# A graph network kernel's prologue: weight loads behind adj and x, layernorm of batch 1 ahead of the branch, VectorE's work dealt anew

## The chip, the cores and the metric

The kernel runs on one core of a Trainium2 chip. The metric is the device time of one execution in microseconds (us). Before the change it was 1216.17 us, the median of three runs (1215.86 to 1218.9). All runs below are in the fast state. A ratio is the mean time of one kernel's fast runs divided by that of the other's fast runs of the same rounds on the same chip, with a 95% interval; it is therefore not quite the ratio of the medians quoted beside it.

Engines in the profile: PE is TensorE, PEld its weight loads, DVE VectorE, ACT ScalarE, POOL GpSimd, SP SyncE. "L442" is a line of that kernel's own source, so the same statement has another number in each kernel.

## The reference

There are 32 batches of x, each 512 rows by 512 features, and one 512x512 matrix adj, all fp32.

```python
# layer 0
h = jnp.maximum(_layernorm(x), 0.0)
x = x + (einsum('nm,bmd->bnd', adj, h) @ weight + bias)
# layer 1: attention, masked by (1 - adj) * -1e9, 8 heads
h = jnp.maximum(_layernorm(x), 0.0)
x = x + (softmax(scores + mask) @ v) @ Wo + bo
```

adj is sparse with values up to 1, so the mask is close to one-hot per row. The kernel finds the largest entry of each row of adj, checks with bounds from the weights that the softmax picks just that row, and then replaces attention by a gather of rows (the "single path"); otherwise it branches to a general path. The inputs here take the single path.

## The kernel before

The prologue runs before the branch. adj goes out in four chunks on SyncE's queue, batch 0 of x on ScalarE's, the weights right behind them on the same two queues, and three bias vectors on GpSimd's queue:

```python
for c in range(C):
    nc.sync.dma_start(mask[:, c, :], adj[c * P:(c + 1) * P, :])
    nc.scalar.dma_start(xs[0][:, c, :], x[0, c * P:(c + 1) * P, :])
# ... constants ...
for t, v in zip(bt, (bq, bk)):
    nc.gpsimd.dma_start(t, v.rearrange("(c p) -> p c", p=P))
nc.gpsimd.dma_start(b0_r, ...)          # bias, one row copied to 128 partitions
load_w(nc.scalar, wt[0], wq)
load_w(nc.sync, wt[1], wk)
load_w(nc.scalar, w0_s, w0)
load_w(nc.sync, xs[1], x[1])
load_w(nc.scalar, wv_s, wv)
load_w(nc.sync, wo_s, wo)
```

TensorE transposes the chunks of adj as they land, ScalarE and VectorE copy the transposes from PSUM, and then TensorE aggregates batch 0 over features (24 passes, two more products, the row counts). A check value decides the branch.

After the branch every 512x512x512 product is done as seven half-size pieces (Strassen's way), whose operand sums VectorE makes: h0s for the aggregation, yTs for layer 0. While TensorE works on one piece, a list of steps says what the other engines do. Batch 0's part of that list:

```python
for c in range(C):
    put(0, c, add_b0, c)
for step, i in ((0, 0), (0, 1), (0, 2), (1, 3)):
    put(0, step, lambda b, i: sum_b(adjT_s, adjT, i), i)
for step, c in ((1, 0), (1, 1), (2, 2), (2, 3)):
    put(1, step, lambda b, c: first[0].stats(c), c)      # layernorm of batch 1
put(1, 2, lambda b: first[0].power())
put(1, 3, lambda b: first[0].offset())
for c in range(C):
    put(1, 3, lambda b, c: first[0].relu(c), c)
for step, i in ((3, 0), (7, 1), (8, 2), (9, 3)):
    put(1, step, h0_sum, i)
# ... number_rows at 9, list_rows at 10 to 13, w0_t sums at 15 to 17 ...
run(layer0_rows(0), todo[0:4])            # batch 0, layer 0
run(aggregate(b + 1), todo[7:14])         # batch 1, aggregation in seven pieces
run(fold_weights(), todo[14:21])          # Wv x Wo
```

So the aggregation of batch 1 needs a layernorm, a ReLU and the sums h0s that VectorE makes only after the branch.

## Time and profile before

| | before |
|---|---|
| time, first three runs | 1216.17 us median |
| profiled span | 1217.6 us |
| TensorE busy | 1164.6 us, 96% of the span |
| aggregation of batch 0 starts | 12.71 us |
| first product after the branch (layer 0 of batch 0) | 31.71 us |
| layer 0 of batch 1 starts | 81.81 us |
| mean granted clock of TensorE | 0.988 |

TensorE is the bound, so only the time in which it waits, or in which it runs at half clock, can be won. The start of layer 0 of batch 1 is a good milestone: from there both kernels issue the same instructions in the same order, and a lead there should reach the end. The page's groups show the largest single wait of the one kind that the change attacks (columns: busy us, mean ns, idle before and its releaser):

```profile
L271 PE MATMUL mm<-adjT_s,h0s 128*128 128x256 f32 x744 | 171.0, 379 | 3.8 <-DVE h0s L248 3.2
```

Of 744 passes in 31 batches, one waits 3.2 us for h0s: only batch 1's.

### The profile page before, as it was taken

The numbers are of one execution on the slowest core, as the hardware profiler recorded it, in microseconds if no ns is written. First come the engines' busy times: TensorE is split into PE (matmuls) and PEld (weight loads), VectorE is DVE, ScalarE is ACT, GpSimd is POOL, SyncE is SP. The second block draws the span as 40 slices with busy tenths as digits, with TensorE's granted clock in tenths as the row PEclk, the third lists the DMA queues.
The fourth block names the chain that finished last, engine by engine and source line by source line (L and its number), as shares of the span: only waits on it lengthen the run. The fifth ranks groups of instructions, "written<-read, shape, count | busy, mean of one in ns | idle before, by whom it ended". The sixth has DMA issues, their size and how long they took to land.

```text
span 1217.6 us, 14536 instructions
## 1 busy us (share of the span) xinstructions
PE 1164.6 (96%) x5164; PEld 938.2 (77%) x5164; DVE 849.0 (70%) x1854; ACT 327.3 (27%) x499; POOL 401.9 (33%) x340
## 2 busy tenths in 40 slices
PE   7899999999999999999999999999999999999971
PEld 3458888888888888888888888888888888888841
DVE  4877776777777677777767777777777777777541
ACT  3223223222322322232232223223222322322110
POOL 1132432433233343324324332433433243343332
PEclk9999999999999999999999999999999999999986
DMA  8222665565566556556655655665565566555466
GB/s 284 78 61 91 169 169 147 152 188 167 152 169 167 149 152 186 169 152 167 167 149 152 185 170 152 168 168 148 152 186 170 153 166 171 144 152 153 135 162 149
DMA packets 97874, 192.43 MB, mean 158 GB/s; under 512 B 10624, under 2 KB 10624, under 8 KB 97792
## 3 DMA queue, kind: packets, MB, share of 16 engines
q1 hardware_dynamic: 69104, 127.95, 28.7%
q0 software_dynamic: 26528, 59.27, 26.6%
q10 hardware_dynamic: 2160, 4.19, 0.9%
q8 instruction: 42, 0.69, 0.2%
q14 instruction: 40, 0.33, 0.1%
HBM read 99.10 MB, written 92.28 MB: 157 GB/s over the span
## 4 chain that ended last, share of the span: by engine, by line
PE 86%; DVE 7%; DMA 1%; issue 1%; POOL 1%; ACT 0%; SPq 0%; POOLq 0%; DVEq 0%; ACTq 0%
PE mm L271 72%; PE mm L478 9%; PE pt L464 3%; DVE st L185 2%; DVE zs L482 2%; PE mm L352 1%; DVE zs L318 1%; DVE mv L186 1%; DMA hc<-hs,listed 1%; POOL x L488 0%; DMA z<-zs 0%; DVE x L422 0%; ACT h L199 0%; DVE x L445 0%; DVE yT L308 0%
## 5 line engine op out<-in xcount | busy, mean ns | idle before, releaser
L488 POOL DMA_INDIRECT x<-z,place x128 | 201.5, 1574 | 252.0 <-DMA z<-zs 209.6
L199 ACT ACTIVATE h<-x,off,rstd 128x512 f32<-128x512 f32 x256 | 194.7, 807 | 201.9 <-DVE off L195 201.9
L326 DVE TENSOR_TENSOR x<-mm,x 128x512 f32<-128x512 f32 x217 | 149.8, 690 | 119.1 <-PE mm L271 119.1
L192 POOL TENSOR_TENSOR rstd<-ve,mhalf 128x2 f32<-128x2 f32 (+1 forms) x97 | 88.2, 909 | 288.4 <-DVE ve L191 287.0
L185 DVE BATCH_NORM_STATS2 st<-x 128x6 f32<-128x512 f32 x256 | 175.3, 685 | 10.9 <-DMA x<-in_x_dram 8.7
L455 POOL DMA_INDIRECT hc<-hs,listed x96 | 102.8, 1071 | 235.3 <-PE mm L271 177.5
L271 PE MATMUL mm<-adjT_s,h0s 128*128 128x256 f32 x744 | 171.0, 379 | 3.8 <-DVE h0s L248 3.2
L271 PE MATMUL mm<-w_t,sel 128*128 128x256 f32 x744 | 171.0, 379 | 1.2 <-DVE x L326 1.2
L271 PEld LDWEIGHTS mm<-adjT_s,h0s 128*128 128x128 f32 x744 | 141.2, 190 | 23.6 <-issue 4.5
L271 PEld LDWEIGHTS mm<-w_t,sel 128*128 128x128 f32 x744 | 138.9, 190 | 19.1 <-DVE x L326 1.6
L465 ACT COPY hT<-pt 128x512 f32<-128x512 f32 x96 | 56.5, 588 | 356.3 <-PE pt L464 356.3
L310 ACT COPY yT<-mm 128x512 f32<-128x512 f32 x124 | 72.7, 586 | 266.2 <-PE mm L271 222.1
L478 PE MATMUL mm<-wvo,hT 128*128 128x512 f32 x256 | 116.8, 599 | 0.7 <-ACT hT L465 0.7
L271 PE MATMUL mm<-adjT,h 128*128 128x256 f32 x496 | 117.3, 379 | 0.0
L271 PE MATMUL mm<-w_s,yT 128*128 128x256 f32 x496 | 117.2, 379 | 0.0
L308 DVE TENSOR_TENSOR yT<-mm,yT 128x512 f32<-128x512 f32 x93 | 64.3, 692 | 75.2 <-PE mm L271 72.9
L271 PE MATMUL mm<-wvo_t,hTs 128*128 128x256 f32 x384 | 104.2, 395 | 6.5 <-DVE zs L318 6.2
L271 PEld LDWEIGHTS mm<-w_s,yT 128*128 128x128 f32 x496 | 94.2, 190 | 13.2 <-issue 0.5
L271 PEld LDWEIGHTS mm<-adjT,h 128*128 128x128 f32 x496 | 94.1, 190 | 13.3 <-ACT h L199 0.6
L271 PEld LDWEIGHTS mm<-wvo_t,hTs 128*128 128x128 f32 x384 | 67.9, 189 | 32.5 <-DVE zs L318 24.9
L478 PEld LDWEIGHTS mm<-wvo,hT 128*128 128x128 f32 x256 | 49.2, 193 | 49.5 <-issue 46.9
L422 DVE TENSOR_TENSOR x<-x,b_r 128x512 f32<-128x512 f32 x128 | 87.3, 683 | 0.0
(131 smaller groups left out, 1309.1 us busy)
## 6 DMA issues: line engine op xcount, KB each, us to landing
hs<-h SPq DMA_DIRECT2D x64, 512.0 KB
out_dram<-x SPq DMA_DIRECT2D x128, 256.0 KB
x<-in_x_dram SPq DMA_DIRECT2D x120, 256.0 KB
z<-zs SPq DMA_DIRECT2D x96, 256.0 KB
x<-z,place POOLq DMA_INDIRECT x128
hc<-hs,listed POOLq DMA_INDIRECT x96
x<-in_x_dram ACTq DMA_DIRECT2D x4, 256.0 KB
mask<-in_adj_dram SPq DMA_DIRECT2D x4, 256.0 KB
```

Of the source, the lines that this page charges most:

```text
L185: self.nc.vector.bn_stats(st, self.src[:, self.chunks[i], :])
L192: self.nc.gpsimd.tensor_tensor(self.rstd, ve, self.mhalf[:, 0:n], ALU.pow)
L199: self.nc.scalar.activation(self.dst[:, c, :], self.src[:, c, :], AF.Relu, bias=self.off[:, i:i + 1], scale=self.rstd[:, i:i + 1])
L271: nc.tensor.matmul(bank[:, m, :], lhs[:, k, m * P:(m + 1) * P], rhs[:, k, :], start=(first and m == 0 and k == 0), stop=(k == 1), skip_gro ...
L308: nc.vector.tensor_add(dst, bank, dst)
L310: nc.scalar.copy(dst, bank)
L326: nc.vector.tensor_add(dst, bank, dst)
L422: nc.vector.tensor_add(X[b][:, c, :], X[b][:, c, :], b0_r)
L455: nc.gpsimd.indirect_dma_start(out=HC[b][:, r, :], out_offset=None, in_=HS[b], in_offset=bass.IndirectOffsetOnAxis(ap=listed[:, r:r + 1], ...
L465: nc.scalar.copy(HT[b][:, :, r * P:(r + 1) * P], pt)
L478: nc.tensor.matmul(flat, HT[b][:, d, 2 * P:3 * P], wvo[:, d, :], start=(d == 0), stop=(d == DC - 1))
L488: nc.gpsimd.indirect_dma_start(out=X[b][:, c, :], out_offset=None, in_=Z[b], in_offset=bass.IndirectOffsetOnAxis(ap=place[:, c:c + 1], axi ...
```

## The change

Its intent has three parts. Part 1 holds the weight loads back behind adj and x and puts them all on ScalarE's queue. Part 2 does batch 1's layernorm ahead of the branch, where VectorE is idle. Part 3 deals VectorE's work after the branch anew.

```diff
-        load_w(nc.scalar, wt[0], wq)
-        load_w(nc.sync, wt[1], wk)
-        load_w(nc.scalar, w0_s, w0)
-        if B > 1:
-            load_w(nc.sync, xs[1], x[1])
-        load_w(nc.scalar, wv_s, wv)
-        load_w(nc.sync, wo_s, wo)
...
-        for i in range(2):
+        for i, w in enumerate((wq, wk)):
             norms[0].relu(i)
+            load_w(wt[i], w)
...
         for i in range(2):
             norms[1].relu(i)
+        if B > 1:
+            load_w(xs[1], x[1])
+        for t, w in ((w0_s, w0), (wv_s, wv), (wo_s, wo)):
+            load_w(t, w)
...
+        if B > 1:
+            norms.append(Norm(nc, small, mhalf, xs[1], hs[1], range(C)))
+            norms[2].stats(0)
+            norms[2].stats(1)
...
+            if d == 3 and B > 1:
+                norms[2].relu(0)
+                norms[2].relu(1)
             nc.scalar.copy(yT[:, d, :], ps)
...
                 nc.vector.tensor_scalar_min(used, few[:, 0, :], 1.0)
+                if B > 1:
+                    norms[2].stats(2)
+                    norms[2].stats(3)
+                    norms[2].power()
+                    norms[2].offset()
+        if B > 1:
+            norms[2].relu(2)
+            norms[2].relu(3)
... (after the branch: the layernorm steps of batch 1 go, the rest gets other steps)
-                for step, i in ((3, 0), (7, 1), (8, 2), (9, 3)):
-                    put(1, step, h0_sum, i)
+            for step, i in ((0, 0), (1, 1), (2, 2), (3, 3)) if b > 0 else ((1, 0), (2, 1), (2, 2), (3, 3)):
+                put(b + 1, step, h0_sum, i)
-                put(0, 9, lambda b: number_rows())
+                put(0, 11, lambda b: number_rows())
+                for step, i in ((11, 0), (12, 1), (12, 2), (13, 3)):
+                    put(0, step, lambda b, i: sum_b(w0_t, w0_s, i), i)
-                    put(0, 10 + m, lambda b, m: list_rows(m), m)
-                put(0, 13, lambda b: end_list())
+                    put(0, 14 + m // 2, lambda b, m: list_rows(m), m)
+                put(0, 16, lambda b: end_list())
```

## The prediction

> **What bounds the kernel now.** I read the page's busy table and chain of waits, then the timeline of each engine for the first 125 us, the only stretch the diff edits.
>
> ```profile
> PE 1164.6 (96%) x5164; PEld 938.2 (77%) x5164; DVE 849.0 (70%) x1854; ACT 327.3 (27%) x499; POOL 401.9 (33%) x340
> ...
> PE 86%; DVE 7%; DMA 1%; issue 1%; POOL 1%; ACT 0%; SPq 0%; POOLq 0%; DVEq 0%; ACTq 0%
> ```
>
> TensorE is busy for 96% of the span, so only its gaps can be won: 1217.6 - 1164.6 = 53 us, of which a good 20 lie behind 1193 us, where its last matmul starts. The gaps of the prologue, from the timeline of TensorE (start, length, and in brackets the idle time and its releaser):
>
> ```profile
> 4.42 3.48 PE L99 MATMUL pt<-ident,mask 128*128 128x128 f32 x12 [4.42 <-DMA mask<-in_adj_dram]
> 11.56 1.12 PE L99 MATMUL pt<-ident,mask 128*128 128x128 f32 x4 [3.66 <-DMA mask<-in_adj_dram]
> 12.71 12.93 PE L138 MATMUL mm<-adjT,h 128*128 128x512 f32 x24
> ...
> 31.71 13.97 PE L442 MATMUL mm<-w_s,yT 128*128 128x512 f32 x32 [1.18 <-DVE before L163]
> 45.52 1.96 PE L271 MATMUL mm<-adjT,h 128*128 128x256 f32 x8
> 48.10 1.97 PE L271 MATMUL mm<-adjT_s,h0s 128*128 128x256 f32 x8 [0.62 <-issue]
> 53.23 1.96 PE L271 MATMUL mm<-adjT_s,h0s 128*128 128x256 f32 x8 [3.16 <-DVE h0s L248]
> 55.56 0.49 PE L381 MATMUL pt<-upper,ones 128*128 128x128 f32 x2 [0.37 <-POOL upper L378]
> ...
> 64.24 0.83 PE L400 MATMUL pt<-ones,hit 128*128 128x1 f32 x6 [0.83 <-DVE hit L395]
> ```
>
> The last quarter of adj lands at 11.56, which stops TensorE for 3.66 us. After the branch the aggregation of batch 1 waits for VectorE, whose chain is layernorm of batch 1, ReLU (44.35 to 47.3), then the sums h0s. VectorE meanwhile sits idle before the branch:
>
> ```profile
> 26.46 0.16 DVE L147 TENSOR_SCALAR used<-few 128x4 f32<-128x4 f32 x1 [3.71 <-PE few L146]
> 28.63 0.16 DVE L149 TENSOR_REDUCE rows<-many 128x1 f32<-128x4 f32 x1 [2.00 <-PE many L137]
> ```
>
> The third view is DMA traffic by queue, here from 7 to 8 us (packets, MB, share of the 16 engines):
>
> ```profile
> q0 software_dynamic: 58, 0.10, 44.8%
> q10 hardware_dynamic: 56, 0.11, 37.5%
> q1 hardware_dynamic: 50, 0.10, 30.1%
> ```
>
> q0 is GpSimd's queue with the three biases (L81, L82), which the change leaves alone; it holds 45% of the engines for a third of the bytes. From 8 to 9 us it holds 56% and all queues move 223 GB/s, from 11 to 12 us, without it, 408 GB/s.
>
> **What the Trainium skill says.** "DMA: Bandwidth & Descriptors", section Queues, rings and completion order: each DMA engine takes turns between the queues that have work, and takes one queue's descriptors in ring order. The trace agrees: pairs of adj and x chunks land at 4.4, 5.6 and, for adj, 6.8 us, about 1.2 us apart, though Wk was issued at 4.30 and Wq at 4.49; the single packet records show no weight completing before adj. So weights issued later on the same two queues do not overtake adj and x; the biases do. Section Anatomy of one DMA: a wait is made on the issuing sequencer. The trace agrees: ScalarE's issue of Wv stood until 8.29, when x's third chunk landed, and its table load started only at 8.70. "TensorE: Matmul & The Clock Gate", section What's actually happening: the clock is halved until a window of about 3.4 us was busy. The trace agrees: weight loads of L138 follow 0.85 us apart until 17.14, then 0.43. "VectorE: DVE Perf Modes", section on the TRN2 errata: an fp32 tensor-tensor add of 512 takes 691 ns; the trace has 690 (L326), and 0.60 us from start to start.
>
> **Part 1, the loads.** Wq and Wk go out after batch 0's first two ReLUs, x[1], W0, Wv, Wo after its last, all on ScalarE's queue. adj and x keep their place, and so do the biases. By ring order I expect the last adj chunk again at about 11.5 and the aggregation at 12.7: gain 0. ScalarE pays about 0.4 us per issue (0.39 in the timeline). First two: x chunk 2 at 8.29 puts the offset at 9.25, so two ReLUs (1.52) and two issues (0.8) end near 11.7, before the transposed adj is wanted at 12.07: free. Last four: 15.64 + 1.6 = 17.3, before the copy at 18.81: free. Arrival, estimated at 390 GB/s and in order: Wq and Wk by 17.3, x[1] by 20, W0 by 22.7, Wo by 28. x[1] is wanted at 22.8, W0 at 32.
>
> **Part 2, layernorm of batch 1 ahead of the branch.** VectorE's two first statistics (0.80 each in the chain) fill the 3.71 us gap. The other two and the variance come after `used`: 26.62 + 1.90 (the same five instructions, 49.12 to 51.02) = 28.52; GpSimd's power on 128x4 takes 1.02, which with handovers makes 29.7; offset to 29.9. Only then comes `rows`, at 28.63 before. Its chain to `sure` takes 0.99, so 30.85 instead of 29.62; but the matmul that needs it started at 30.34 anyway, behind others. Cost: about 0.55 us. ScalarE's two early ReLUs (to 31.5) delay the last yT copy to 32.1, just inside. L442 starts at about 32.3 instead of 31.71.
>
> **Part 3, VectorE after the branch.** Moved out: four statistics, 3.2 us, plus power and ReLU waits. I placed the new order at 0.60 us per 128x512 operation from 34.55 (33.96 + 0.55 + handover), statistics 0.80. h0s is complete at 44.3, before TensorE ends L442 at 32.3 + 13.8 = 46.1, so these gaps go (start minus the start before and its 1.73 us of passes): 48.10 - 47.25 = 0.85, 53.23 - 49.83 = 3.40, 55.56 - 54.96 = 0.60 for `upper`, and 0.08 at 58. TensorE then runs from 46.1 through five pieces of 1.73, c22 the last, to 54.7, and the counting matmuls (0.87) to 55.6. Two gaps come anew. The piece c22 is taken only after number_rows (1.13) and one w_t sum (0.60): 55.6 + 1.13 + 0.60 + 0.68 = 58.0, while c12 ends at 57.3, so the last piece, c21, waits 0.75 and ends at 59.8. The list of rows moved later on both engines: VectorE ends `hit` at about 66.8, TensorE's first fold group at 62.2 + 3.43 = 65.6: a wait of 1.2, where the old one was 0.99. The 62.2 is 59.8 plus 2.29 for the transposes of Wv (64.93 to 67.22 before) plus 0.2 for a ScalarE copy that now stands ahead of them. After `hit` come its matmuls (0.69), three fold groups (10.3) and the bias product (0.85): 66.8 + 11.85 = 78.7.
>
> Sum: gained 0.85 + 3.40 + 0.60 + 0.08 + 0.99 = 5.92; lost 0.75 + 1.20 + 0.20 = 2.15; lost before the branch 0.55. Net 3.2 us. Layer 0 of batch 1 starts near 78.7 instead of 81.81, which the placed order gives too (3.1). From there the order of instructions is the same on every engine, so the lead is carried to the end: 1216.2 - 3.2 = 1213.0.
>
> **Rivals.** (a) adj and x do land sooner without weights: at the earlier pace of 1.2 us the last pair is due at 8.0. For it: the stall begins at 6.4, some 2 us after the first weight issue. Against it: ring order, and q0's share. Even then ScalarE (ReLU, issue, ReLU, issue, copies) holds the aggregation until about 10.9, so at most 1.8 us more: 1211. (b) VectorE's order after the branch is worse than placed, the new gaps eat the old ones, and the time stays at 1215 to 1216. For it: VectorE is 92 and 95% busy in the slices 30 to 40 and 50 to 60 us. Against it: the 3.2 us of statistics really leave. (c) The late yT copy or a late x[1] delays the branch by 1 to 3 us: 1214 to 1216. Against it: 2.8 us of slack for x[1].
>
> **Range and chances.** 3.2 us is 0.3%, and even all of (a) on top leaves under 0.6%, while 2% is 24 us. The three runs before spread over 3 us, and the clock window can shift by a microsecond or two. Hence 1210.3 to 1215.6, and within 2% nearly surely.
>
> **What would show it.** Right: adj's last chunk near 11.5, L442 near 32.3, no wait for h0s around 50, one wait of about a microsecond for `hit` near 66, layer 0 of batch 1 near 78.7. Wrong: the last chunk at 8 to 9; a wait of TensorE before the branch that names x[1] or ScalarE; a start of layer 0 near 81; or a lead lost after 90 us.

## The result, and the profile after

After the change six runs have a median of 1211.49 us (1210.69 to 1213.36); the kernel before in the same rounds has 1217.62 us. The ratio is 0.9951, interval 0.9937 to 0.9965, so 6.0 us (0.0049 of 1217.6), within 2% as predicted and inside the range, but with almost twice the gain of 3.2 us that was worked out (from 4.3 to 7.7 by the interval). The stated time was met closely (1211.49 against 1213.0) in part because the three first runs of before lay 1.4 us low.

The page of the changed kernel, busy time and chain of waits:

```profile
PE 1164.2 (96%) x5164; PEld 938.5 (78%) x5164; DVE 848.6 (70%) x1854; ACT 327.1 (27%) x499; POOL 402.0 (33%) x340
...
PE 90%; DVE 7%; DMA 1%; issue 1%; POOL 1%; SPq 0%; ACT 0%; POOLq 0%; ACTq 0%; DVEq 0%
```

No engine does less or more work: VectorE's 848.6 us were 849.0. Work only moved, and TensorE's part of the last chain rose from 86 to 90%. The timeline of TensorE in the prologue and after the branch (start, length, idle time and releaser in brackets):

```profile
4.42 3.47 PE L91 MATMUL pt<-ident,mask 128*128 128x128 f32 x12 [4.42 <-DMA mask<-in_adj_dram]
9.97 1.12 PE L91 MATMUL pt<-ident,mask 128*128 128x128 f32 x4 [2.08 <-DMA mask<-in_adj_dram]
11.13 11.76 PE L139 MATMUL mm<-adjT,h 128*128 128x512 f32 x24
...
29.30 13.97 PE L452 MATMUL mm<-w_s,yT 128*128 128x512 f32 x32 [1.18 <-ACT yT L145]
...
54.97 1.99 PE L283 MATMUL mm<-adjT_s,h 128*128 128x256 f32 x8 [0.67 <-DVE yT L320]
...
63.91 0.80 PE L410 MATMUL pt<-ones,hit 128*128 128x1 f32 x6 [1.20 <-DVE hit L405]
74.95 1.02 PE L369 MATMUL mm<-part,ones 128*128 128x512 f32 x2
```

The last chunk of adj lands at 9.97 instead of 11.56. The first product after the branch starts at 29.30 instead of 31.71, so before the branch this pair of profiles shows 2.41 us won. Part of that is one execution's luck: before_warm and before_warm2 below leave this prologue as it was and reach the branch at 31.36 and 30.22. The bias product stands at 74.95 (80.96 before), and layer 0 of batch 1 starts 0.86 us later, at 75.81 instead of 81.81: 6.00 us of lead, 3.59 of them after the branch. The wait for h0s is gone, and waits for yT (0.67; the aggregated features, which layer 0 multiplies next) and for `hit` (1.20; a step of the list of rows) have come. The lead is carried: the last product of the second-last layer 1, near the end of the span, starts at 1165.79 against 1171.86, a lead of 6.07. The span differs by 8.6 us only because the last few microseconds happened to go better in this profile (TensorE's last product starts 25.7 us before the end of before's span and 22.3 us before the end of after's); we put that down to noise of one execution. The runs' means show 6.0 as well, but that both figures agree is partly chance: the profile of before has a slow prologue, and lacks an effect that many of its other executions have (see loads_only).

VectorE's idle time ahead of the branch, which was 3.71 and 2.00 us, is what Part 2 filled (timeline of VectorE):

```profile
23.70 0.16 DVE L151 TENSOR_SCALAR used<-few 128x4 f32<-128x4 f32 x1 [0.93 <-PE few L150]
26.81 0.16 DVE L207 SCALAR_TENSOR_TENSOR off<-mv,rstd 128x4 f32<-128x4 f32 x1 [1.12 <-POOL rstd L204]
```

And the group that had waited 3.2 us for h0s:

```profile
L283 PE MATMUL mm<-adjT_s,h0s 128*128 128x256 f32 x744 | 170.7, 379 | 0.0
```

So two questions are open. Why did adj land sooner, against the argument from ring order, and what is that worth? And is the rest of the gain the layernorm, the new deal, or something else? The theory to begin with is that the late loads brought adj forward and with it the missing microseconds. The rivals are TensorE's clock, and an effect of the removed wait beyond its length.

### The profile page after: what moved, and what is told of

It reads as the page before. It is cut to its first block, busy times and chain, and to the rows that moved or that the text cites. A ratio compares the mean times of both kernels' runs of the same rounds, so it can differ in the third digit from the quotient of the medians.

```text
span 1209.0 us, 14537 instructions
## 1 busy us (share of the span) xinstructions
PE 1164.2 (96%) x5164; PEld 938.5 (78%) x5164; DVE 848.6 (70%) x1854; ACT 327.1 (27%) x499; POOL 402.0 (33%) x340
## 3 DMA queue, kind: packets, MB, share of 16 engines
q1 hardware_dynamic: 67520, 124.81, 28.1%
## 4 chain that ended last, share of the span: by engine, by line
PE 90%; DVE 7%; DMA 1%; issue 1%; POOL 1%; SPq 0%; ACT 0%; POOLq 0%; ACTq 0%; DVEq 0%
PE mm L283 74%; PE mm L488 9%; PE pt L474 4%; DVE st L197 2%; DVE zs L492 2%; PE mm L452 1%; PE mm L139 1%; PE mm L364 1%; DVE zs L330 1%; DMA mask<-in_adj_dram 1%; DVE mv L198 1%; DMA hc<-hs,listed 0%; POOL x L498 0%; DMA z<-zs 0%; DVE x L338 0%
```

## The experiments

All runs gave correct results. Every experiment had five rounds. The table takes the milestones from each run's profile; "br" is the start of the first product after the branch, and the last column is the time from there to the first product of layer 1 that reads the sums hTs.

| kernel | ratio, interval | median us | adj's last chunk | aggregation | br | br to layer 1 |
|---|---|---|---|---|---|---|
| before | | 1217.4 (27 runs, first call) | 11.56 | 12.71 | 31.71 | 81.35 |
| after | 0.9951, 0.9937–0.9965 | 1211.49 | 9.97 | 11.13 | 29.30 | 77.70 |
| loads_only | 0.9996, 0.9986–1.0006 | 1216.97 | 10.10 | 11.31 | 29.92 | 84.21 |
| loads_undone | 0.9961, 0.9947–0.9974 | 1212.16 | 11.02 | 12.17 | 30.18 | 77.71 |
| bias_late | 0.9997, 0.9988–1.0006 | 1217.10 | 8.45 | 11.21 | 30.07 | 81.29 |
| after_bias_late | 0.9956, 0.9943–0.9969 | 1211.57 | 8.33 | 10.50 | 30.22 | 77.71 |
| norm_only | 0.9962, 0.9948–0.9975 | 1212.60 | 10.98 | 12.13 | 31.45 | 77.47 |
| before_warm | 1.0009, 0.9999–1.0018 | 1218.34 | 11.22 | 12.37 | 31.36 | 83.13 |
| before_warm2 | 0.9991, 0.9981–1.0001 | 1215.91 | 11.01 | 12.16 | 30.22 | 81.37 |
| after_warm | 0.9945, 0.9932–0.9959 | 1210.14 | 10.32 | 11.27 | 28.53 | 77.71 |
| deal | 0.9929, 0.9915–0.9943 | 1208.38 | 10.30 | 11.45 | 30.37 | 75.09 |
| deal_warm | 0.9927, 0.9913–0.9940 | 1208.06 | 10.24 | 11.19 | 28.57 | 75.09 |
| best | 0.9935, 0.9922–0.9947 | 1209.51 | 10.98 | 11.92 | 29.97 | 75.08 |
| best2 | 0.9955, 0.9941–0.9969 | 1210.69 | 8.49 | 10.56 | 29.98 | 75.08 |

(The column of landing is the start of the transposes of that chunk. In after_warm, deal_warm and best idle products stand ahead of them, so the chunk itself landed sooner.)

### loads_only: Part 1 alone

```diff
 (kernel before)
+ Wq, Wk issued on ScalarE's queue after batch 0's first two ReLUs,
+ x[1], W0, Wv, Wo after its last two; nothing else changed
```

> The kernel before with Part 1 of the change alone: weights and x[1] issued late, on ScalarE's queue, layernorm and VectorE's order as before. Theory W (weights in flight do slow the last chunk of adj): the last chunk lands near 10.0 as in the changed kernel, the aggregation starts near 11.1 instead of 12.7, ratio 0.9975 to 0.999. Rival B (only the biases on GpSimd's queue delay it, and the 1.6 us was chance): it lands at 11.3 to 11.6, ratio 1.000.

The median is 1216.97 us, the ratio 0.9996. The chunk lands sooner, at 10.10, and yet no time is measurably won: the interval leaves at most 1.7 us, so the theory that the late loads brought all of the missing 2.8 us falls. The profile of this kernel also shows something that the profiled execution of before did not (timeline of TensorE after the branch):

```profile
51.44 2.38 PE L268 MATMUL mm<-adjT_s,h0s 128*128 128x256 f32 x8 [3.16 <-DVE h0s L245]
...
55.07 3.76 PE L268 MATMUL mm<-adjT,h 128*128 128x256 f32 x8
```

After the wait of 3.16 us the eight passes at 55.07 take 3.76 us, where the same eight took 1.97 in before: TensorE is at half clock, and the clock's record has it so from 52.9 to 59.7, 6.83 us. The stretch from the branch to layer 1 takes 84.21 us instead of 81.35. If the wait is the cause, it can thus cost 2.9 us more than its own length. That is a new theory, followed up in before_warm and before_warm2.

### loads_undone: the change without Part 1

```diff
 (kernel after)
- weight loads behind the ReLUs, on ScalarE's queue
+ weight loads right behind adj and x, as before
```

> The changed kernel with Part 1 undone: weights and x[1] issued early on two queues. Theory W: the last chunk lands at 11.5 again, the row-wise layer 0 starts near 32.1 (0.35 later than before the change), layer 0 of batch 1 starts 3.2 us earlier than before, near 78.6, ratio 0.9970 to 0.9980. Rival B: as the changed kernel, 0.995.

The ratio is 0.9961: 4.7 us of the gain (0.0039 of 1217.5) need no change of the loads at all. Against 0.9951 of the whole change that leaves 1.2 us for Part 1, with intervals that overlap; together with 0.5 us from loads_only the worth of Part 1 is somewhere between nothing and a good microsecond. The intervals do not settle it.

### bias_late and after_bias_late: the bias loads moved instead

```diff
 (kernel before, and kernel after)
-        for t, v in zip(bt, (bq, bk)):                       # at the start
-            nc.gpsimd.dma_start(t, ...)
-        nc.gpsimd.dma_start(b0_r, ...)
         norms[1].power()
+        for t, v in zip(bt, (bq, bk)):
+            nc.gpsimd.dma_start(t, ...)
+        nc.gpsimd.dma_start(b0_r, ...)
```

> The kernel before with the three bias loads moved behind the second power on GpSimd, weights early as before. Rival B: the last chunk of adj lands at 8.0, the aggregation starts near 10, ratio 0.997 to 0.9985. Theory W in its strict form (weights alone take the bandwidth): it still lands at 9.5 or later. If both share the blame it lands between 8.0 and 9.5.

> The changed kernel with the three bias loads moved behind the second power as well. Both theories: with neither weights nor biases in flight the last chunk lands at 8.0 (pace of 1.2 us per pair), ScalarE's ReLUs and copies then hold the aggregation until about 10.0 instead of 11.1, ratio to the kernel before 0.9935 to 0.9945, 1 us better than the change.

The biases are most of what delays adj. Without them in flight it lands at 8.45 with the weights early and at 8.33 with the weights late; with them it lands at 11.0 to 11.6 with the weights early (five profiles) and at 10.0 to 10.3 with the weights late (three, leaving out those with idle products ahead). DMA traffic by queue from 7 to 8 us (packets, MB, share of the 16 engines), first the kernel after, then bias_late:

```profile
q10 hardware_dynamic: 72, 0.15, 47.6%
q1 hardware_dynamic: 70, 0.14, 37.6%
q0 software_dynamic: 54, 0.06, 23.3%
```

```profile
q1 hardware_dynamic: 103, 0.18, 56.8%
q10 hardware_dynamic: 112, 0.20, 52.7%
```

GpSimd's queue, q0, is gone from that window in bias_late, and the two others move 0.38 MB instead of 0.29 (0.21 in before, as the prediction shows). The weights matter too, but only while the biases are in flight: early weights add about 1 us then, and next to nothing when the biases are late. The packet counts show that weights do get ahead of adj. adj is 576 packets, 1.05 MB: in after, where nothing else is on SyncE's queue (q1), the count stops there. In before, q1 has started 591 packets (1.09 MB) by 10 us and 744 (1.39 MB) by 11.56, when the last chunk lands; so some 0.3 MB of weights went out on that queue before adj was complete. The order of the queue thus held at most within each of the 16 engines, not across them. The records don't name the engine, so how those weights slow the rest of adj stays open; q0's share is smaller with the weights late (23.3% against 44.8%).

Yet the sooner landing is worth no measurable time: 0.9997 and 0.9956. The timeline of TensorE in bias_late says why:

```profile
8.45 1.11 PE L96 MATMUL pt<-ident,mask 128*128 128x128 f32 x4 [0.39 <-DMA mask<-in_adj_dram]
11.21 12.76 PE L138 MATMUL mm<-adjT,h 128*128 128x512 f32 x24 [1.64 <-ACT adjT L110]
```

First, the aggregation now waits 1.64 us for ScalarE's copy of the transposed adj, which stands behind the layernorm. Second, the 24 passes take 12.76 us. In after_bias_late they start at 10.50, the earliest start of all kernels here, and take 13.27. At full clock they need 10.3 (24 of 0.43 us); the rest, 2.5 and 3.0 us, is what half clock added. Full clock came at 15.7 and 16.0 us in these two profiles, at 17.5 in before and 13.6 in after: it does not follow the start of the work. In these profiles an earlier start therefore buys mostly passes at half speed. Late biases also have a side effect, which counts in best2 below: in after_bias_late VectorE waits 2.63 us for x[1], to 22.26 us, where it had landed by 20.0 in after. There it cost nothing yet, as VectorE then waits for TensorE's row counts anyway.

### norm_only: layernorm ahead, old deal of VectorE

```diff
 (kernel before)
+ norms[2]: statistics, power, offset and ReLU of batch 1 in the prologue, as in the change
- its steps after the branch
  all other steps, and the loads, as before
```

> The kernel before with the layernorm of batch 1 ahead of the branch and nothing else: loads early, VectorE's other work after the branch in the old steps. Theory N (the wait for the sums is what counts): the wait of 3.16 us is gone or under 1, layer 0 of batch 1 starts near 78.5 to 79.5 by the profile, ratio 0.9965 to 0.9975, so the re-deal adds under 0.5 us. Rival D (the re-deal is needed to win it): a wait for h0s of 1.5 us or more stays, ratio 0.998 to 0.999.

The ratio is 0.9962, the same as loads_undone, which has the new deal on top. TensorE after the branch:

```profile
49.14 1.97 PE L286 MATMUL mm<-adjT_s,h0s 128*128 128x256 f32 x8 [0.27 <-DVE h0s L263]
...
76.87 1.02 PE L372 MATMUL mm<-part,ones 128*128 128x512 f32 x2
```

The wait of 3.16 us for h0s shrank to 0.27 with the old order. The stretch from the branch to layer 1 takes 77.47 us, and 77.70 in after. So the layernorm ahead is the gain after the branch, and dealing VectorE's work anew adds nothing to it: it removes small waits and makes others as large. The cost before the branch can be read too: from the aggregation to the branch norm_only takes 19.32 us and before took 19.00.

### before_warm and before_warm2: the wait kept, TensorE kept busy in it

```diff
 (kernel before, product(), batch 1's piece "u2" only; shortened: the count is passed in as warm=26)
             elif piece == "u2":
+                pt = ps_t.tile([P, DC, P], F32, name="pt")
+                for _ in range(26):            # before_warm2: 13
+                    nc.tensor.matmul(pt[:, 0, :], ones, ident, start=True, stop=True)
                 bank = u
```

> The kernel before with 26 dummy matmuls (some 2.9 us) in TensorE's wait for the sums h0s, so that the wait stays but TensorE is not idle. Theory C (the wait costs more than its length, since in some runs it drops TensorE to half clock for a window of 6.8 us around 50 us): no run has a mean granted clock under 0.988, the mean falls by 0.7 to 1.5 us, the spread of the runs shrinks from 5 to 3 us, ratio 0.9988 to 0.9995. Rival R (the low clocks come from elsewhere): clocks from 0.985 to 0.989 as before, ratio 1.000.

before_warm missed its aim. Its 26 products are 52 passes and took 5.97 us, longer than the wait, so the next piece started late and the stretch grew from 81.35 to 83.13 us. The ratio of 1.0009 says nothing about the clock. Its clock readings are a partial miss too: two of 14 are 0.987, where none below 0.988 was expected. The repeat has half as many:

> The kernel before with 13 idle products (26 passes of 0.115 us, an estimate of 3.0 us from the 5.97 us that 52 took in before_warm) in the wait for h0s, which was 3.16 us. The last time there were twice as many and they outlasted the wait. Theory (TensorE's wait halves the clock afterwards in about half of the executions, and so costs more than its length): every run has a mean granted clock of 0.988 or 0.989 as in the kernels without the wait, and the median falls to that of the fast half of the runs of the kernel before, 1215.4 to 1217.8, so a ratio of 0.998 to 0.9995. Rival (the wait costs its length and no more; the spread of clocks has another cause): clocks from 0.985 to 0.989 as before, ratio 1.000 within 0.001.

```profile
48.42 3.06 PE L286 MATMUL pt<-ident,ones 128*128 128x128 f32 x26
51.74 1.97 PE L271 MATMUL mm<-adjT_s,h0s 128*128 128x256 f32 x8 [0.26 <-DVE h0s L248]
```

Now the idle work fits, and the stretch is 81.37 us, unchanged against 81.35. But the granted clock changed. Of 75 executions of the kernel before in all rounds, 46 had a mean clock of 0.985 to 0.987, with a mean time of 1217.9 us, and 29 had 0.988 or 0.989, with 1216.7. Of the 14 of before_warm2 none was below 0.988; loads_only and bias_late, which keep the wait, have ten and seven of 14 below it. The mean over the span doesn't say where the half clock lies, and most of it lies in the last 40 us of every profile (from 1178 us in before), so 0.987 is no sharp border, as before_warm's two show. But none of the 28 executions with the wait filled has 0.986 or less, and 31 of the 75 have. So the wait for h0s, where TensorE sits idle in it, lowers the clock in some four to six executions of ten. What that is worth in time is not settled: the mean fell by 1.15 us (1216.37 against 1217.52 in the same rounds), and the interval of the ratio just touches 1 (from 0.1 us lost to 2.3 won). Likewise none of the 31 executions of norm_only, loads_undone, after_bias_late, after_warm, deal and deal_warm, and none of the six of after, had a clock below 0.988.

### after_warm: idle products in the prologue

```diff
 (kernel after)
+        idle = ps_l.tile([P, N], F32, name="mm", bufs=2)
         for c in range(C):
+            for _ in range((13, 1, 1, 8)[c]):
+                nc.tensor.matmul(idle[:, 0:P], ones, ident, start=True, stop=True)
             for m in range(C):
                 nc.tensor.transpose(pts[m][:, c, :], mask[:, c, m * P:(m + 1) * P], ident)
```

> The changed kernel with 23 dummy matmuls on TensorE before and between the first transposes, so that its clock is full when the aggregation of batch 0 begins. Theory C: the aggregation's 24 passes take 10.4 us instead of 11.8 and the time falls by 1.2 to 2.5 us against the changed kernel, ratio 0.9930 to 0.9942. Rival: no gain (0.995), if the first clock window depends on other things or the branch waits for ScalarE.

```profile
1.57 5.37 PE L92 MATMUL mm<-ident,ones 128*128 128x128 f32 x26 [1.57 <-POOL mhalf L77]
...
11.27 10.84 PE L142 MATMUL mm<-adjT,h 128*128 128x512 f32 x24 [0.35 <-ACT adjT L106]
```

Full clock came at 6.21 us, and the 24 passes took 10.84 us instead of 11.76. The branch is reached at 28.53, 0.77 us sooner than in after's profile. The ratio went from 0.9951 to 0.9945; the direction fits, the size lies within the intervals.

### deal: a third deal of VectorE's work

```diff
 (kernel after)
-                put(0, 11, lambda b: number_rows())
-                for step, i in ((11, 0), (12, 1), (12, 2), (13, 3)):
+                put(0, 9, lambda b: number_rows())
+                for step, i in ((10, 0), (14, 1), (15, 2), (16, 3)):
                     put(0, step, lambda b, i: sum_b(w0_t, w0_s, i), i)
-                    put(0, 14 + m // 2, lambda b, m: list_rows(m), m)
-                put(0, 16, lambda b: end_list())
+                    put(0, 11 + m // 2, lambda b, m: list_rows(m), m)
+                put(0, 13, lambda b: end_list())
- the four sums of wvo_t right behind the fold of Wv and Wo
+ the same in batch 1's steps 4, 5 and 10
- get_h of batch 0 in step 17
+ get_h of batch 0 in step 16
```

> The changed kernel with a third deal of VectorE's work: numbering of rows at step 9, list of rows at 11 and 12, W0's sums after it, the sums of Wvo in the idle time of batch 1. My placement of the waits says that the three gaps of the changed kernel (0.67 for yT, 1.20 for hit, 1.13 for x) go: 2.5 to 3.0 us, ratio 0.9925 to 0.9935. Rival (VectorE is full, gaps only move): under 1 us, 0.9945 to 0.995.

The ratio is 0.9929, 1208.38 us. The waits for yT, `hit` and x (0.67, 1.20 and 1.13 us in after) are gone and one of 0.68 for ScalarE has come, so the stretch to layer 1 takes 75.09 us instead of 77.70, 2.6 us less; the ratio fell by 0.0022, 2.7 us. A lead after the branch does reach the end.

```profile
59.25 1.09 PE L356 MATMUL pt<-ident,x 128*128 128x128 f32 x8 [0.68 <-ACT zs L357]
...
74.82 1.02 PE L369 MATMUL mm<-part,ones 128*128 128x512 f32 x2
```

### deal_warm, best and best2: can all of it be had together?

deal_warm is deal with after_warm's idle products. best adds the late biases of bias_late. best2 mends best in two places:

```diff
-            for _ in range((13, 1, 1, 8)[c]):
+            for _ in range((13, 1, 1, 2)[c]):
...
-        for t, w in ((w0_s, w0), (wv_s, wv), (wo_s, wo)):
+        for t, w in ((w0_s, w0), (wv_s, wv)):
             load_w(t, w)
+        nc.sync.dma_start(wo_s, wo.rearrange("(c p) o -> p c o", p=P))
```

> The kernel after with the third deal of VectorE's work (0.9929 alone) and the idle products of the prologue (0.9945 alone, against 0.9951 of the kernel after). If the two add up: 0.9929 - 0.0006 = 0.9923, some 1207.7 us. Rival: a warmer start brings a product ahead of VectorE again, its gaps come back by as much, ratio 0.993.

> As deal_warm, and the bias loads behind the second layernorm's power step, so that the last chunk of adj lands near 8.4 instead of 10.3 while the clock is already full. Theory (an earlier landing yields nothing in bias_late only because TensorE runs at half clock then): the aggregation starts 0.5 to 1.5 us earlier, as far as ScalarE's copies of adjT allow (1.05 us of wait in after_bias_late), ratio 0.991 to 0.992. Rival (the landing is worth nothing whatever the clock, as ScalarE's copies or the layernorm take over): same ratio as deal_warm within 0.0005.

> Kernel best mended in two places: two idle products instead of eight ahead of the last chunk (there they ran from 9.19 to about 11 us, past the landing of the chunk), and Wo loaded over SyncE's queue behind adj, as its issue held ScalarE for 4.15 us and TensorE for 0.64 us. Theory (earlier landing of adj is worth time once TensorE is at full clock and ScalarE is free): the aggregation starts at 9.5 to 10.8 us instead of 11.92 (best) and 11.19 (deal_warm) and has no wait inside; ratio 0.991 to 0.9925, against 0.9927 of deal_warm. Rival (the copies of adjT behind the layernorm's reciprocal root, done at about 11.0 in deal_warm, hold it all the same, or fewer idle products leave the clock at half): start of 11 us or later, ratio 0.9925 to 0.994.

deal_warm has the best measured median, 1208.06 us, ratio 0.9927; it beats both kernels, though against deal alone (0.9929) the difference is too small to call. best came out at 0.9935, no better: its last eight idle products held the transposes of the last chunk back to 10.98, and the issue of Wo on ScalarE's queue took 4.15 us and held ScalarE and then TensorE (0.64 us). In best2 that was mended (Wo's issue on SyncE's queue took 0.38 us), adj landed by 8.49 and the aggregation started at 10.56 as the theory said, already at full clock (from 5.16). Still the branch is reached at 29.98, later than the 28.57 of deal_warm, and the ratio of 0.9955 is worse than both the theory and its rival gave. TensorE, ScalarE, then VectorE in best2:

```profile
10.56 7.13 PE L143 MATMUL mm<-adjT,h 128*128 128x512 f32 x16 [1.42 <-ACT adjT L106]
18.62 3.70 PE L143 MATMUL mm<-adjT,h 128*128 128x512 f32 x8 [0.92 <-ACT yT L149]
...
28.44 0.19 PE L175 MATMUL few<-ones,sure 128*1 128x1 f32 x2 [1.35 <-DVE sure L174]
```

```profile
17.79 0.20 ACT L145 ACTIVATE bt<-bt 128x4 f32<-128x4 f32 x1 [5.22 <-DMA bt<-in_L_gnn_bq_dram]
18.00 0.56 ACT L149 COPY yT<-mm 128x512 f32<-128x512 f32 x1
```

```profile
22.60 0.69 DVE L201 BATCH_NORM_STATS2 st<-x 128x6 f32<-128x512 f32 x1 [2.80 <-DMA x<-in_x_dram]
```

ScalarE sits idle for 5.22 us for the bias bq, which now stands behind the weights, and its copy of yT, next in its program, cannot free the PSUM buffer that TensorE wants: 0.92 us. But the last four aggregation passes then start at 25.13, only 0.17 us later than in deal_warm (24.96). The rest of the delay of 1.41 us comes behind them, and it comes from x[1]: VectorE waits 2.80 us for it, so batch 1's layernorm and the chain to `sure`, the check value, end later, and TensorE waits 1.35 us for that value where deal_warm waited 0.28. x[1] lands at 22.3 to 22.6 us in the three kernels with late biases and late weights (after_bias_late, best, best2), and at 20.0 to 21.0 in five with early biases and late weights (after, loads_only, after_warm, deal, deal_warm). So moving the biases out of the way of adj puts them in the way of x[1] (after and after_bias_late differ in nothing else) and delays bq; the branch is no sooner. These 1.4 us are less than half of the 3.4 by which best2's ratio is worse than deal_warm's; the rest is not explained. Three of best2's six executions (0.985 to 0.987) and two of best's six (0.987) also had a clock below 0.988, which, apart from before_warm's two, no other kernel without the idle wait for h0s showed; which of their waits does it was not tried.

## Why the prediction was right or wrong

**What bounds the kernel: right.** TensorE's busy time hardly moved (1164.6 and 1164.2 us), and the lead at the milestone, 6.00 us, was carried to the last batch, 6.07.

**Part 1, "the last adj chunk again at about 11.5 … gain 0": the landing was wrong, the gain about right.** The step that failed is the inference from ring order. It said that the packet records show no weight completing before adj; the counts show some 0.3 MB of weights on SyncE's queue by 11.56 us, before adj was complete. So weights queued behind adj, together with the biases, do delay it: 9.97 instead of 11.56. The biases were named correctly as the larger cause (8.45 without them in flight). Rival (a) had the direction of the landing, though not the size (8.0); its "at most 1.8 us more" overstates what it brings: loads_only (0.9996) and loads_undone (0.9961 against 0.9951) give 0.5 and 1.2 us. TensorE's half clock and ScalarE's copies take up the rest in the profiles. The cost on ScalarE was mis-sized too: the last four issues took 4.09 us (0.38, 0.52, 0.73 and 2.46) instead of 1.6, which held nothing up in after. The arrivals came as estimated (x[1] at 20.0, W0 at 22.7, Wo at 28.1).

**Part 2, 0.55 us before the branch: right in kind, a little large.** From the start of the last four aggregation passes to the branch before took 3.26 us (28.45 to 31.71) and after 3.61 (25.69 to 29.30), so 0.35; norm_only shows 0.32 over the whole aggregation. The last copy of yT, called just inside, ended at 28.99 and is what the profile names as the releaser. That `L442 starts at about 32.3` failed for another reason, the landing and the clock: of the 2.41 us won there, 1.58 are the landing and 1.17 the 24 passes (12.93 to 11.76), less 0.35. That 1.17 is only the moment at which full clock came in one execution of each (17.5 and 13.6 us).

**Part 3: right to a tenth.** From the branch to layer 0 of batch 1 the step gave 46.4 us (78.7 less 32.3); it took 46.51 (75.81 less 29.30), and 50.10 before. The new gaps were put at 0.75 for c21, the last piece of the aggregation, and 1.2 for `hit` and measured 0.67 and 1.20. (59.8 + 2.29 + 0.2 is 62.3 and not 62.2, so the sum really gave 1.1 for `hit`.) norm_only (46.28) adds what the prediction did not say: all of it is the layernorm, and the rest of the deal gives as much as it takes. The prediction's own sum has it: apart from the waits for h0s (0.85 and 3.40) it gains 0.60, 0.08 and 0.99, which is 1.67, against 2.15 of new gaps.

**The net of 3.2: right for the waits, and the term left out is, as far as is known, the clock after the wait.** Parts 2 and 3 together measured 3.24 us (3.59 less 0.35) in the pair of profiles, so the sum of the waits came out. But norm_only and loads_undone, which have no faster loads, gain 4.6 and 4.7 us (from 3.0 and 3.2 us upward by their intervals). The term left out is that TensorE's longest wait does not end with its length: in some four to six of ten executions half clock follows, 2.9 us of it where a profile caught it, some 1.15 us in the mean by before_warm2. 3.24 plus 1.15 make 4.4. That the wait brings the half clock is shown by the clocks; that it makes up the missing time fits the numbers, but the intervals don't show it. What remains to the 6.0 of the whole change, some 1.6 us, is Part 1 and noise in shares that these intervals do not separate. The prediction did write that the clock window can shift by a microsecond or two, but held it for noise in the range and not for an effect of the wait that the change removes. It read the 3.40 us for h0s off a profile in which the clock happened to stay up.

**Rivals: (b) did not happen, (c) hardly.** VectorE's order was as placed, and x[1] held nothing up in after. The late yT copy of (c) did come onto the path, for the 0.35 us above. The late x[1] of (c) came in best2, with a branch 1.4 us later than deal_warm's.

## What to carry to other kernels

When TensorE is the bound, price a wait at its length and look at the granted clock of many runs before and after: here a wait of 3.16 us was followed by 6.83 us of half clock in one profile and by a lower mean clock in four to six executions of ten, and another profile missed it. A transfer that lands sooner is worth only what the next wait leaves, here copies on ScalarE and passes at half clock, so follow what stands behind it before moving loads. Filling idle time ahead of a branch with work that a later chain waits for was worth most (4.6 us in norm_only); reordering the rest was worth nothing in the change, and 2.7 us in deal, where it was aimed at the remaining waits one by one.

## What the Trainium skill lacked or had wrong

- "TensorE: Matmul & The Clock Gate", section HAM oscillation, gives the rule "no PE-idle gaps >~3.4µs". Here a wait of 3.16 us with smaller ones near it (0.62 us ahead of it in the timeline of before) was enough: 31 of 75 executions had a clock of 0.986 or less, and none of 28 once the wait was filled. (The page's closing table says some 3 µs, which these runs fit.) The half clock of 6.83 us in loads_only is twice the window of 3413 ns that its section What's actually happening states. That section lets the moment of full clock vary by 500 ns, and adds only that the number of slow products differs between runs; in the kernels without idle products full clock came about 2 us (loads_undone) to 5.5 us (after_bias_late) after the aggregation's start, in one profile each.
- "DMA: Bandwidth & Descriptors", section Queues, rings and completion order, has the round-robin, with which the trace agrees (58, 56 and 50 packets of the three queues in one microsecond of before), but no figure for what small loads on GpSimd's queue cost the others. Here three bias loads took 44.8% of the engines' time in one microsecond, for a third of the bytes, and delayed the last chunk of adj from 8.45 to 11.56 us.
- No page that I read has a figure for how the issue of a DMA grows when large loads were issued just before it on the same queue: the issue of Wo on ScalarE's queue, 1 MB behind three other loads of 1 MB, took 2.46 us in after and 4.15 in best, where Wq's took 0.39 in both, and 0.38 on SyncE's queue in best2.
